# Row-LSTM over a 128x128 image: channels 64-95 of x beside the state h, gates kept in PSUM, GpSimd held until VectorE's reads end, four engines' orders written down

## The chip, the cores and the metric

The kernel runs on one core of a Trainium2 chip. The metric is the device time of one execution in microseconds (us); lower is better. Besides the time, one execution was taken by the hardware profiler; all rows quoted below come from its page and its trace. PE is TensorE's matrix multiply, PEld its weight load, DVE is VectorE, ACT is ScalarE, POOL is GpSimd, SP is SyncE, whose queue issues the DMAs of the loop.

## The reference

```python
# x: (8, 96, 128, 128) = batch, channels, rows, columns
def step(carry, row_in):                       # lax.scan over the 128 rows
    h, c = carry                               # (8, 96, 128) each
    ss = conv1d(h, W_ss, kernel 3, padding 1) + b_ss
    gates = ss + row_in                        # 384 channels
    f, i, o, g = sigmoid, sigmoid, sigmoid, tanh of the four quarters
    c_new = f * c + i * g
    h_new = o * jnp.tanh(c_new)
    return ((h_new, c_new), h_new)

its = conv(group_norm(x), W_is * mask, 1x3) + b_is   # the mask leaves the left tap and a part of the middle one
x = x + scan(step, zeros, its by rows)
```

The rows are a recurrence: row r+1 needs the h of row r. The eight images are independent of each other.

## The kernel before

**Statistics.** The kernel first reads x once (64 DMAs) and takes mean and variance of each channel with VectorE's BN_STATS; two small matmuls sum them by group.

**The recurrence.** The batch is cut into two streams `s` of four images. A step of one stream for one row, here a half-step, handles 96 channels x 4 images x 128 columns. There are 256 of them: 32 blocks `k` of `R` = 4 rows, times two streams, issued alternately, so that one stream's tail can lie beside the other's start. Columns are split in even and odd ones (`J` = 64 each), and the three-tap convolution is computed from three inputs: `vs` = even + odd, `vf` = odd - even, and `vd`, two shifted differences. For each of three gate groups `a`, taken in the order 1, 0, 2, TensorE multiplies `vs` and `vf` into the two halves of one PSUM bank `ps[a]` (called *both* below), ScalarE copies the low half with the bias added into `m` (L258), VectorE writes sum and difference back over the two halves (L259, L260: the *sums*), and TensorE adds three more products on top, from `xn` and twice from `vd` (the *rest*). Every product appears as two matmul records. A bank holds 96 partitions of one sigmoid gate (group 0 is f, 1 is i, 2 is o) and 32 partitions of a third of g.

After the rests ScalarE takes tanh of the g parts (L269) and sigmoid of the others (L270) into SBUF tiles `sf`, `si`, `so`; VectorE forms sf*c (L272), si*g (L273), the new c (L274) and, after ScalarE's tanh of c (L275), h = so*th (L279). From h it makes the next row's `vs` and `vf` (L286, L287), and GpSimd makes `vd` (L288) and adds h onto the rows of x that are stored (L294).

**Inputs from x.** Partitions 96-127 of `vs`, `vf`, `vd` and of the weights hold channels 64-95 of the normalised x, so that they ride along in the same matmuls; GpSimd fills them one block ahead, once per row and stream (L198 normalises, L231 and L232 make sum and difference). Channels 0-63 go into `xn` (L198, L217), also by GpSimd. The buffers hold a whole block of four rows and there are two of each.

**What sets the order.** GpSimd's order is that of the code. The orders of TensorE, ScalarE and VectorE are chosen by the scheduler of the tile framework. All DMAs of the loop are issued by SP: `load_rows` (two copies of 512 KB into `xr`, one buffer per stream), `load` (256 KB and 768 KB into one of two buffers of x) and `store` (768 KB).

Of the kernel before, what the change touches and what calls it, by code (L numbers as in the profile page):

```python
# [7 lines left out]
F32 = mybir.dt.float32  # L8
# [13 lines left out]
def kernel(  # L22
# [26 lines left out]

    nc = tc.nc  # L50
    B, C, H, W = x.shape
    P = 128
# [22 lines left out]

    wt = const.tile([P, 5, 4 * C], F32, name="wt")
    wr = const.tile([P, 3, 4 * C], F32, name="wr")
    nc.scalar.dma_start(wr[0:C], w_ss)
# [15 lines left out]
    nc.vector.tensor_add(wr[0:C, 0, :], wr[0:C, 0, :], wr[0:C, 2, :])  # L94
    nc.vector.tensor_add(wt[0:C, 1, :], wr[0:C, 0, :], wr[0:C, 1, :])
    nc.vector.tensor_sub(wt[0:C, 2, :], wr[0:C, 0, :], wr[0:C, 1, :])
    nc.vector.tensor_scalar_mul(wt[0:C, 1:3, :], wt[0:C, 1:3, :], 0.5)
    nc.vector.tensor_scalar_mul(wt[C:P, 1, :], wr[C:P, 1, :], 0.5)
    nc.vector.tensor_scalar_mul(wt[C:P, 2, :], wr[C:P, 1, :], -0.5)
# [17 lines left out]
    vd = pair([P, R, 2, BH, JP], "vd")  # L117
    vs = pair([P, R, BH, J], "vs")
    vf = pair([P, R, BH, J], "vf")
    xn = pair([P, R, 2, BH, J], "xn")  # L120

    hh = pair([C, 2, BH, JP], "hh")
    xr = [const.tile([P, BH, R * W + 1], F32, tag=f"xr{s}", name=f"xr{s}") for s in range(NH)]
    cs = [const.tile([C, 2, BH, J], F32, tag=f"c{s}", name=f"c{s}") for s in range(NH)]
    for s in range(NH):
        nc.gpsimd.memset(cs[s], 0.0)
        nc.gpsimd.memset(xr[s][:, :, 0:1], 0.0)
        nc.gpsimd.memset(vs[s][0][0:C, 0], 0.0)
        nc.gpsimd.memset(vf[s][0][0:C, 0], 0.0)
        nc.gpsimd.memset(vd[s][0][0:C, 0], 0.0)  # L130
        for i in range(2):
            nc.gpsimd.memset(hh[s][i][:, 0, :, J : J + 1], 0.0)
            nc.gpsimd.memset(hh[s][i][:, 1, :, 0:1], 0.0)
            nc.gpsimd.memset(vd[s][i][C:P, :, 1, :, 0:1], 0.0)
# [84 lines left out]
    def normalise_shared(s, k, j):  # L219

        i = k % 2
        z = vd[s][i][C:P]
        norm(
            strided(z[:, 0, 0, j, :], 0, [(2 * BH * JP, R), (BH * JP + 1, 2), (1, J)]),
            xt[s, k][C:P, j, :, :].rearrange("p r (j t) -> p r t j", t=2),
            C,
            0,
            s * BH + j,
        )
        e, o = z[:, :, 0, j, 0:J], z[:, :, 1, j, 1 : J + 1]  # L230
        nc.gpsimd.tensor_add(vs[s][i][C:P, :, j, :], e, o)  # L231
        nc.gpsimd.tensor_sub(vf[s][i][C:P, :, j, :], o, e)  # L232

    def step(s, k, r):
        i = k % 2
        order = (1, 0, 2)
        HB = BH * J
        ps = [
            ps_pool.tile([P, 2 * HB], F32, tag=f"ps{a}", name=f"ps{a}_{s}_{k}_{r}")
            for a in range(3)  # L240
        ]
        flat = "p b j -> p (b j)"

        def mm(a, half, p, rhs, start=False, stop=False):
            o = ps[a] if half is None else ps[a][:, bass.ts(half, HB)]
# [3 lines left out]

        def gt(n, shape=(C, 2 * HB)):  # L250
            return g_pool.tile(list(shape), F32, tag=n, name=f"{n}_{s}_{k}_{r}")

        for a in order:
            mm(a, 0, 1, vs[s][i][:, r].rearrange(flat), start=True)
            mm(a, 1, 2, vf[s][i][:, r].rearrange(flat))
            m1 = gt(f"m{a}", (P, HB))
            lo, hi = ps[a][:, 0:HB], ps[a][:, HB : 2 * HB]
            nc.scalar.activation(m1, lo, AF.Identity, bias=bias[:, a : a + 1])  # L258
            nc.vector.tensor_add(lo, m1, hi)  # L259
            nc.vector.tensor_sub(hi, m1, hi)  # L260
        for a in order:
            mm(a, None, 4, xn[s][i][:, r].rearrange("p t b j -> p (t b j)"))
            mm(a, 0, 0, vd[s][i][:, r, 1, :, 0:J])
            mm(a, 1, 3, vd[s][i][:, r, 0, :, 0:J], stop=True)

        sg = [gt("sf"), gt("si"), gt("so")]
        g, th = gt("g"), gt("th")
        for a in order:
            nc.scalar.activation(g[a * 32 : (a + 1) * 32], ps[a][C:P], AF.Tanh)  # L269
            nc.scalar.activation(sg[a], ps[a][0:C], AF.Sigmoid)  # L270
        c = cs[s].rearrange("p t b j -> p (t b j)")
        nc.vector.tensor_mul(sg[0], sg[0], c)  # L272
        nc.vector.tensor_mul(g, sg[1], g)  # L273
        nc.vector.tensor_add(c, sg[0], g)  # L274
        nc.scalar.activation(th, c, AF.Tanh)  # L275
        h = hh[s][r % 2]
        h3 = strided(h[:, 0, 0, :], 0, [(BH * JP + 1, 2), (JP, BH), (1, J)])
        shaped = "p (t b j) -> p t b j"
        nc.vector.tensor_mul(  # L279
            h3, sg[2].rearrange(shaped, t=2, b=BH), th.rearrange(shaped, t=2, b=BH)  # L280
        )
        if (k, r) != (NB - 1, R - 1):
            kn, rn = (k, r + 1) if r + 1 < R else (k + 1, 0)
            n = kn % 2
            e, o = h[:, 0, :, 0:J], h[:, 1, :, 1 : J + 1]
# [18 lines left out]
    for s in range(NH):  # L304
        load_rows(s, 0)
        load(s, 0)
# [72 lines left out]
```

## Time and profile before

| quantity | value |
|---|---|
| runs without the profiler | 2945.25, 2950.84, 2955.51 us; median 2950.84 |
| the profiled execution's own time | 2938.35 us |
| its span from first to last instruction | 2936.5 us |
| statistics, up to the first group matmul | 207.28 us |
| first matmul of the recurrence | 224.40 us |
| mean granted TensorE clock | 0.958 |
| mean time from one tanh of c (L275) to the next | 10.55 us |

A line of a group reads: source line, engine, operation, output tile <- input tiles, shapes, count, then the busy time and the mean duration of one in ns, then the time for which the engine was idle just before, with what ended it. A line of the timeline gives start and duration in us, and in brackets the idle time before it. In a timeline line "x2" two records are merged, and a matmul's recorded end is modelled: the distance between the starts of two groups tells the pace better than the durations.

### The profile page before, as it was taken

The page shows a single profiled execution, that of the slowest core. Times are in us where ns is not written, and L with a number is a line of the kernel's source. Part 1 is how long each engine was busy: PE and PEld are TensorE (multiplying, and loading weights), DVE is VectorE, ACT ScalarE, POOL GpSimd, SP SyncE. Part 2 cuts the span into 40 slices and gives each one's busy share as a digit, 9 for nine tenths or more (in the row PEclk, how much of TensorE's full clock was granted, in tenths as well). Part 3 has the DMA queues.
Part 4 walks back from the last instruction along what each step waited for, and adds up shares of the span by engine and source line. Part 5 has one row for each costly group of instructions (what it writes and reads, how often), then busy time and mean ns, then how long its engine had stood idle before and what let it go on. Part 6 is the DMA issues. An engine that isn't in the chain of part 4 may idle for free.

```text
span 2936.5 us, 26168 instructions
## 1 busy us (share of the span) xinstructions
PE 2255.3 (77%) x7688; PEld 1481.7 (50%) x7688; DVE 2074.1 (71%) x3352; ACT 1364.6 (46%) x2564; POOL 1567.7 (53%) x1828
## 2 busy tenths in 40 slices
PE   0008888888888888888888888888888888888887
PEld 0005555555555555555555555555555555555555
DVE  7876766677766766776666677766777776777666
ACT  0005445445554444554454455544444555454445
POOL 0016555665555556555555655555556555555562
PEclk9999999999999999999999999999999999999999
DMA  9992333312233332122333212233332122333300
GB/s 248 259 255 54 79 79 79 79 43 62 54 79 79 79 79 61 44 66 67 79 79 79 68 45 70 56 79 79 79 79 65 44 69 60 79 79 79 79 22 22
DMA packets 103581, 237.76 MB, mean 81 GB/s; under 512 B 6576, under 2 KB 7088, under 8 KB 97296
## 3 DMA queue, kind: packets, MB, share of 16 engines
q1 hardware_dynamic: 102400, 234.91, 32.7%
q10 hardware_dynamic: 1040, 1.18, 0.2%
q8 instruction: 63, 1.03, 0.1%
q14 instruction: 78, 0.64, 0.1%
HBM read 185.73 MB, written 50.33 MB: 80 GB/s over the span
## 4 chain that ended last, share of the span: by engine, by line
DVE 46%; PE 21%; POOL 18%; DMA 5%; ACT 5%; issue 4%; ACTq 0%; POOLq 0%; DVEq 0%
PE ps L246 21%; DVE vf L287 9%; DVE ps L259 8%; DVE vs L286 7%; DVE ps L260 6%; DVE hh L279 6%; DMA xc<-in_x_dram 5%; POOL vd L198 5%; DVE g L273 4%; DVE c L274 4%; POOL vs L231 4%; ACT g L269 4%; POOL x L294 3%; POOL xn L198 2%; POOL vd L288 2%
## 5 line engine op out<-in xcount | busy, mean ns | idle before, releaser
L246 PE MATMUL ps<-xn,wt 128*128 128x512 f32 x1536 | 842.1, 630 | 250.7 <-DVE ps L260 249.4
L269 ACT ACTIVATE g<-ps 32x512 f32<-32x512 f32 x768 | 454.2, 591 | 953.2 <-PE ps L246 953.1
L288 POOL TENSOR_TENSOR vd<-hh 96x512 f32<-96x512 f32 x254 | 263.7, 1038 | 1082.3 <-DVE hh L279 1082.3
L246 PEld LDWEIGHTS ps<-vd,wt 128*128 128x128 f32 x3072 | 582.2, 190 | 411.7 <-issue 370.6
L246 PE MATMUL ps<-vd,wt 128*128 128x256 f32 x3072 | 788.2, 378 | 0.0
L246 PE MATMUL ps<-vs,wt 128*128 128x256 f32 x1536 | 522.5, 425 | 212.0 <-POOL vs L231 212.0
L258 ACT ACTIVATE m<-ps,bias 128x256 f32<-128x256 f32 x768 | 358.0, 466 | 386.6 <-PE ps L246 385.8
L246 PE MATMUL ps<-vf,wt 128*128 128x256 f32 x1536 | 517.6, 422 | 0.0
L259 DVE TENSOR_TENSOR ps<-m,ps 128x256 f32<-128x256 f32 x768 | 309.4, 422 | 274.1 <-ACT m L258 274.1
L246 PEld LDWEIGHTS ps<-xn,wt 128*128 128x128 f32 x1536 | 253.0, 191 | 468.9 <-DVE ps L260 454.9
L246 PEld LDWEIGHTS ps<-vs,wt 128*128 128x128 f32 x1536 | 320.6, 213 | 287.0 <-POOL vs L231 237.4
L273 DVE TENSOR_TENSOR g<-si,g 96x512 f32<-96x512 f32 x256 | 176.3, 689 | 300.4 <-ACT g L269 300.4
L294 POOL TENSOR_TENSOR x<-x,hh 96x512 f32<-96x512 f32 x256 | 377.3, 1474 | 14.1 <-DVE hh L279 14.1
L287 DVE TENSOR_TENSOR vf<-hh 96x256 f32<-96x256 f32 x254 | 380.7, 1499 | 0.0
L246 PEld LDWEIGHTS ps<-vf,wt 128*128 128x128 f32 x1536 | 324.0, 213 | 68.1 <-POOL vf L232 19.7
L198 POOL TENSOR_SCALAR xn<-xr,rstd,nmr 128x512 f32<-128x512 f32 x256 | 247.8, 968 | 199.0 <-DVE nmr L176 198.9
L272 DVE TENSOR_TENSOR sf<-sf,c 96x512 f32<-96x512 f32 x256 | 178.4, 697 | 218.9 <-ACT sf L270 218.9
L260 DVE TENSOR_TENSOR ps<-m,ps 128x256 f32<-128x256 f32 x768 | 325.4, 424 | 8.9
L286 DVE TENSOR_TENSOR vs<-hh 96x256 f32<-96x256 f32 x254 | 294.0, 1157 | 0.0
L231 POOL TENSOR_TENSOR vs<-vd 32x256 f32<-32x256 f32 x256 | 247.5, 967 | 21.3
L198 POOL TENSOR_SCALAR vd<-x,rstd,nmr 32x512 f32<-32x512 f32 x256 | 235.5, 920 | 23.4
L274 DVE TENSOR_TENSOR c<-sf,g 96x512 f32<-96x512 f32 x256 | 207.1, 809 | 8.9
(49 smaller groups left out, 1187.5 us busy)
## 6 DMA issues: line engine op xcount, KB each, us to landing
xr<-in_x_dram SPq DMA_DIRECT2D x128, 512.0 KB, 6.9
xc<-in_x_dram SPq DMA_DIRECT2D x64, 768.0 KB, 9.6
x<-in_x_dram SPq DMA_DIRECT2D x64, 768.0 KB, 9.8
out_dram<-x SPq DMA_DIRECT2D x64, 768.0 KB, 5.3
x<-in_x_dram SPq DMA_DIRECT2D x64, 256.0 KB, 7.3
wr<-in_w_ss_dram ACTq DMA_DIRECT2D x1, 432.0 KB, 7.9
wt<-in_w_ss_dram ACTq DMA_DIRECT2D x2, 144.0 KB, 10.0
wt<-in_w_is_dram ACTq DMA_DIRECT2D x2, 96.0 KB, 4.2
```

The lines of the kernel that those rows point to most:

```text
L198: nc.gpsimd.tensor_scalar(dst, src, rstd[lo:P, layout, b : b + 1], nmr[lo:P, layout, b : b + 1], ALU.mult, ALU.add,)
L231: nc.gpsimd.tensor_add(vs[s][i][C:P, :, j, :], e, o)
L246: nc.tensor.matmul(o, wt[:, p, bass.ts(a, P)], rhs, start=start, stop=stop, skip_group_check=True)
L258: nc.scalar.activation(m1, lo, AF.Identity, bias=bias[:, a : a + 1])
L259: nc.vector.tensor_add(lo, m1, hi)
L260: nc.vector.tensor_sub(hi, m1, hi)
L269: nc.scalar.activation(g[a * 32 : (a + 1) * 32], ps[a][C:P], AF.Tanh)
L274: nc.vector.tensor_add(c, sg[0], g)
L286: nc.vector.tensor_add(vs[s][n][0:C, rn], e, o)
L287: nc.vector.tensor_sub(vf[s][n][0:C, rn], o, e)
L288: nc.gpsimd.tensor_sub(vd[s][n][0:C, rn, :, :, 0:J], strided(h[:, 0, 0, :], 1, [(BH * JP - 1, 2), (JP, BH), (1, J)]), h3,)
L294: nc.gpsimd.tensor_add(xr_, xr_, h3)
```

## The change

There are four edits, and some setup that follows from them.

1. **Channels 64-95 of x treated as channels of h.** `vd`, `vs`, `vf` (for whole blocks) and `hh` go. In their place `hx` holds h in partitions 0-95 and the normalised channels 64-95 of x in partitions 96-127, per row. One pair of VectorE instructions on 128 partitions makes `vs` and `vf` for both, and one GpSimd instruction makes `vd`; the GpSimd sum and difference for x alone (L231, L232) are gone. The weights get rows for it: the right tap of partitions 96-127 is zero.
2. **Gates kept in PSUM.** The sigmoids are written in place into `ps[a]`; the products f*c, i*g, the sum c and the output h read one operand from there. `sf`, `si`, `so` are gone.
3. **GpSimd held.** The GpSimd instruction that makes `vd` gets an added dependence on VectorE's `vf`.
4. **Orders written down.** TensorE, ScalarE, VectorE and GpSimd follow the code. A half-step `now` is interleaved with the end of the one before it, `prev`, which is the other stream's. GpSimd's normalisation is spread over the rows in another way (`OWN`, `SHARED`), and the loads are written stream by stream: blocks 0 and 1 before the loop, block k+2 at the end of block k, where it was the start of block k+1 for both streams together.

```diff
-    for p, tap in ((0, 0), (3, 2)):
-        nc.scalar.dma_start(wt[0:C, p, :], w_ss[:, tap])
-        nc.scalar.dma_start(wt[C:P, p, :], w_is[C2:C, 0])
+    nc.scalar.dma_start(wt[0:C, 3, :], w_ss[:, 2])
+    nc.gpsimd.memset(wt[C:P, 3, :], 0.0)
...
+    hx = pair([P, R, 2, BH, JP], "hx")
...
-        e, o = z[:, :, 0, j, 0:J], z[:, :, 1, j, 1 : J + 1]
-        nc.gpsimd.tensor_add(vs[s][i][C:P, :, j, :], e, o)
-        nc.gpsimd.tensor_sub(vf[s][i][C:P, :, j, :], o, e)
...
+    def inputs(s, row):
+        h = hx[s][row // R % 2][:, row % R]
+        vs, vf = gt("vs", s, row, (P, HB)), gt("vf", s, row, (P, HB))
+        vd = gt("vd", s, row, (P, 2, HB))
+        shaped = "p (b j) -> p b j"
+        e, o = h[:, 0, :, 0:J], h[:, 1, :, 1 : J + 1]
+        nc.vector.tensor_add(vs.rearrange(shaped, b=BH), e, o)
+        last = nc.vector.tensor_sub(vf.rearrange(shaped, b=BH), o, e)
+        diff = nc.gpsimd.tensor_sub(
+            vd.rearrange("p t (b j) -> p t b j", b=BH),
+            strided(h[:, 0, 0, :], 1, [(BH * JP - 1, 2), (JP, BH), (1, J)]),
+            strided(h[:, 0, 0, :], 0, [(BH * JP + 1, 2), (JP, BH), (1, J)]),
+        )
+        tc.add_manual_dep(
+            diff.ins,
+            last.ins.name,
...
+        def sigmoid(self, a):
+            gate = self.ps[a][0:C]
+            nc.scalar.activation(gate, gate, AF.Sigmoid)
+        def forget(self):
+            f = self.ps[0][0:C]
+            nc.vector.tensor_mul(f, f, cs[self.s].rearrange("p t b j -> p (t b j)"))
+        def gated(self):
+            nc.vector.tensor_mul(self.g, self.ps[1][0:C], self.g)
...
+            self.moving = inputs(s, row + 1) if row + 1 < NT else None
+            xo = xt[s, row // R][0:C, :, row % R, :].rearrange("p b (j t) -> p t b j", t=2)
+            nc.gpsimd.tensor_add(xo, xo, h)
...
+    OWN, SHARED = ((0, 1), (2,), (), (3,)), ((), (0, 1), (2, 3), ())
+    def finish(s, row):
+        prepare(s, row)
+        k = row // R
+        if row % R == R - 1:
+            if k + 2 < NB:
+                load_rows(s, k + 2)
+            store(s, k)
+            if k + 2 < NB:
+                load(s, k + 2)
...
+    with tc.manual_schedule(engines={E.PE, E.Activation, E.DVE, E.Pool}):
+        prev = None
+        for row in range(NT):
             for s in range(NH):
+                now = HalfStep(s, row, moving[s])
+                a0, a1, a2 = order
+                now.both(a0)
+                if prev:
+                    prev.tanh(a2)
+                    prev.gated()
+                now.copy(a0)
+                now.sums(a0)
+                if prev:
+                    prev.sigmoid(a2)
+                now.both(a1)
+                now.copy(a1)
+                if prev:
+                    prev.cell()
+                now.sums(a1)
+                now.both(a2)
+                now.copy(a2)
+                now.sums(a2)
+                if prev:
+                    prev.cell_tanh()
+                    prev.output()
+                    moving[prev.s] = prev.moving
+                    finish(prev.s, prev.row)
+                now.rest(a0)
+                now.tanh(a0)
+                now.sigmoid(a0)
+                now.rest(a1)
+                now.tanh(a1)
+                now.sigmoid(a1)
+                now.forget()
+                now.rest(a2)
+                prev = now
```

In the changed kernel `copy`, `sums`, `rest`, `tanh`, `cell` and `cell_tanh` are the instructions of L258, L259 with L260, the products from `xn` and `vd`, L269, L274 and L275 of before; `both` is the pair of products from `vs` and `vf`. TensorE's order of products is the same in both kernels: three *both*, then three *rest*.

VectorE before, in the middle of the recurrence, for one half-step of stream 0 (the four numbers in `ps_0_5_1_3005` are stream, block, row in the block and a running number; the tiles that end in `_5_0_2982` and the like belong to stream 1, one half-step earlier):

```order
L272 TENSOR_TENSOR sf_5_0_2982<-sf_5_0_2982,c_128 96x512
L273 TENSOR_TENSOR g_5_0_2985<-si_5_0_2983,g_5_0_2985 96x512
L274 TENSOR_TENSOR c_128<-sf_5_0_2982,g_5_0_2985 96x512
L259 TENSOR_TENSOR ps_0_5_1_3005<-m_0_5_1_3009,ps_0_5_1_3005 128x256
L259 TENSOR_TENSOR ps_0_5_1_3004<-m_0_5_1_3015,ps_0_5_1_3004 128x256
L260 TENSOR_TENSOR ps_0_5_1_3005<-m_0_5_1_3009,ps_0_5_1_3005 128x256
L279 TENSOR_TENSOR hh_123<-so_5_0_2984,th_5_0_2986 96x2x4x64
L260 TENSOR_TENSOR ps_0_5_1_3004<-m_0_5_1_3015,ps_0_5_1_3004 128x256
L286 TENSOR_TENSOR vs_112<-hh_123 96x256
L287 TENSOR_TENSOR vf_116<-hh_123 96x256
L259 TENSOR_TENSOR ps_0_5_1_3006<-m_0_5_1_3021,ps_0_5_1_3006 128x256
L260 TENSOR_TENSOR ps_0_5_1_3006<-m_0_5_1_3021,ps_0_5_1_3006 128x256
```

VectorE in the changed kernel, the same place (here `ps_0_21_2885` is stream 0, row 21; `ps_1_20` belongs to stream 1's half-step before it):

```order
L304 TENSOR_TENSOR ps_1_20_2830<-ps_1_20_2830,c_114 96x512
L307 TENSOR_TENSOR g_20_2833<-ps_1_20_2831,g_20_2833 96x512
L286 TENSOR_TENSOR ps_0_21_2885<-m_0_21_2892,ps_0_21_2885 128x256
L287 TENSOR_TENSOR ps_0_21_2885<-m_0_21_2892,ps_0_21_2885 128x256
L311 TENSOR_TENSOR c_114<-ps_1_20_2830,g_20_2833 96x512
L286 TENSOR_TENSOR ps_0_21_2884<-m_0_21_2899,ps_0_21_2884 128x256
L287 TENSOR_TENSOR ps_0_21_2884<-m_0_21_2899,ps_0_21_2884 128x256
L286 TENSOR_TENSOR ps_0_21_2886<-m_0_21_2906,ps_0_21_2886 128x256
L287 TENSOR_TENSOR ps_0_21_2886<-m_0_21_2906,ps_0_21_2886 128x256
L325 TENSOR_TENSOR hx_106<-ps_1_20_2832,th_20_2910 96x2x4x64
L241 TENSOR_TENSOR vs_21_2913<-hx_106 128x256
L242 TENSOR_TENSOR vf_21_2914<-hx_106 128x256
```

The sums of gate group 1 moved ahead of the new c, and those of group 2 moved from behind h, `vs` and `vf` to ahead of them: the three instructions that make the next row's input now come last.

GpSimd before, at the end of a block, for row 3 of one stream (`vd_106`, `vs_110` and `vf_114` are block buffers, `x_5_2441` the next block's x):

```order
L288 TENSOR_TENSOR vd_106<-hh_122 96x8x64
L294 TENSOR_TENSOR x_4_1989<-x_4_1989,hh_122 96x2x4x64
L198 TENSOR_SCALAR xn_118<-xr_125,rstd,nmr 128x8x64
L217 MEMSET xn_118 64x4
L198 TENSOR_SCALAR vd_106<-x_5_2441,rstd,nmr 32x4x2x64
L231 TENSOR_TENSOR vs_110<-vd_106 32x4x64
L232 TENSOR_TENSOR vf_114<-vd_106 32x4x64
L198 TENSOR_SCALAR vd_106<-x_5_2441,rstd,nmr 32x4x2x64
L231 TENSOR_TENSOR vs_110<-vd_106 32x4x64
L232 TENSOR_TENSOR vf_114<-vd_106 32x4x64
```

GpSimd in the changed kernel, from row 2 of stream 1 (first three rows) to row 3 of both streams at the end of a block:

```order
L243 TENSOR_TENSOR vd_27_3565<-hx_105 128x512
L332 TENSOR_TENSOR x_6_2813<-x_6_2813,hx_105 96x2x4x64
L194 TENSOR_SCALAR hx_106<-x_7_3249,rstd,nmr 32x4x2x64 x2
L243 TENSOR_TENSOR vd_28_3617<-hx_104 128x512
L332 TENSOR_TENSOR x_6_2755<-x_6_2755,hx_104 96x2x4x64
L194 TENSOR_SCALAR xn_108<-xr_111,rstd,nmr 128x8x64
L213 MEMSET xn_108 64x4
L243 TENSOR_TENSOR vd_28_3675<-hx_106 128x512
L332 TENSOR_TENSOR x_6_2813<-x_6_2813,hx_106 96x2x4x64
L194 TENSOR_SCALAR xn_110<-xr_112,rstd,nmr 128x8x64
```

After the last row of a block there were two normalisations of `vd` with a sum and a difference each; now only one of `xn` and its memset stand there, and the normalisations into `hx` are done by the end of row 2.

More of the change, by code (lines that the diff above doesn't have):

```diff
@@ L248, in mm @@
             )
[L250 to L260, printed above, removed]
@@ L293, in step, with both, copy, sums @@
[L293 to L294 removed]
+        def both(self, a):
+            self.mm(a, 0, 1, self.vs, start=True)
+            self.mm(a, 1, 2, self.vf)
+        def copy(self, a):
+            self.m1 = gt(f"m{a}", self.s, self.row, (P, HB))
+            nc.scalar.activation(
+                self.m1, self.ps[a][:, 0:HB], AF.Identity, bias=bias[:, a : a + 1]
+            )
+        def sums(self, a):
+            lo, hi = self.ps[a][:, 0:HB], self.ps[a][:, HB : 2 * HB]
+            nc.vector.tensor_add(lo, self.m1, hi)
+            nc.vector.tensor_sub(hi, self.m1, hi)
@@ L331 @@
-    for s in range(NH):
-        store(s, NB - 1)
+    for s in range(NH):
+        load_rows(s, 1)
+        load(s, 1)
+    moving = [inputs(s, 0) for s in range(NH)]
+    E = mybir.EngineType
+    with tc.manual_schedule(engines={E.PE, E.Activation, E.DVE, E.Pool}):
+        prev = None
+        for row in range(NT):
+            for s in range(NH):
+                now = HalfStep(s, row, moving[s])
[30 more added lines that the diff above has]
+                prev = now
+        prev.tanh(a2)
+        prev.gated()
+        prev.sigmoid(a2)
+        prev.cell()
+        prev.cell_tanh()
+        prev.output()
+        finish(prev.s, prev.row)
```

148 lines of the change are left out of this document (66 added, 82 removed).

## The prediction

> **What bounds the kernel now.** I read the page first, then the waits, then the timeline of one regular half-step, then that of a block's start.
>
> ```profile
> span 2936.5 us, 26168 instructions
> PE 2255.3 (77%) x7688; PEld 1481.7 (50%) x7688; DVE 2074.1 (71%) x3352; ACT 1364.6 (46%) x2564; POOL 1567.7 (53%) x1828
> DVE 46%; PE 21%; POOL 18%; DMA 5%; ACT 5%; issue 4%; ACTq 0%; POOLq 0%; DVEq 0%
> PEld ps L246 <- DVE ps L260: 454.9, 507, 1.2
> PE ps L246 <- POOL vs L231: 212.0, 64, 14.2
> ```
>
> No engine is full. The chain that ended last is mostly VectorE, though TensorE is the busiest, and TensorE waits for two things: the sums (507 times) and, 64 times, GpSimd's part of `vs` from x. The first is the regular half-step:
>
> ```profile
> 1465.07 0.59 PE L246 MATMUL ps<-vf,wt 128*128 128x256 f32 x2
> 1466.07 0.68 DVE L279 TENSOR_TENSOR hh<-so,th 96x512 f32<-96x512 f32 x1
> 1466.22 1.12 PE L246 MATMUL ps<-xn,wt 128*128 128x512 f32 x2 [0.56 <-DVE ps L260]
> 1466.83 1.04 POOL L288 TENSOR_TENSOR vd<-hh 96x512 f32<-96x512 f32 x1 [3.12 <-DVE hh L279]
> 1467.01 1.15 DVE L286 TENSOR_TENSOR vs<-hh 96x256 f32<-96x256 f32 x1
> 1467.18 1.03 PE L246 MATMUL ps<-vd,wt 128*128 128x256 f32 x4
> 1467.83 1.48 POOL L294 TENSOR_TENSOR x<-x,hh 96x512 f32<-96x512 f32 x1
> 1468.04 1.02 PE L246 MATMUL ps<-xn,wt 128*128 128x512 f32 x2
> 1468.07 1.51 DVE L287 TENSOR_TENSOR vf<-hh 96x256 f32<-96x256 f32 x1
> 1468.90 1.03 PE L246 MATMUL ps<-vd,wt 128*128 128x256 f32 x4
> 1469.51 0.42 DVE L259 TENSOR_TENSOR ps<-m,ps 128x256 f32<-128x256 f32 x1
> 1469.96 0.43 DVE L260 TENSOR_TENSOR ps<-m,ps 128x256 f32<-128x256 f32 x1
> 1470.33 0.10 POOL L217 MEMSET xn<- 64x4 f32 x1
> 1470.45 1.13 PE L246 MATMUL ps<-xn,wt 128*128 128x512 f32 x2 [0.52 <-DVE ps L260]
> 1471.41 1.03 PE L246 MATMUL ps<-vd,wt 128*128 128x256 f32 x4
> 1472.27 0.59 PE L246 MATMUL ps<-vs,wt 128*128 128x256 f32 x2
> 1472.47 0.59 ACT L269 ACTIVATE g<-ps 32x512 f32<-32x512 f32 x1 [1.31 <-PE ps L246]
> 1472.70 0.59 PE L246 MATMUL ps<-vf,wt 128*128 128x256 f32 x2
> 1473.10 0.69 DVE L273 TENSOR_TENSOR g<-si,g 96x512 f32<-96x512 f32 x1 [1.21 <-ACT g L269]
> 1474.26 0.47 ACT L258 ACTIVATE m<-ps,bias 128x256 f32<-128x256 f32 x1 [0.22 <-PE ps L246]
> 1475.58 1.13 PE L246 MATMUL ps<-xn,wt 128*128 128x512 f32 x2 [0.56 <-DVE ps L260]
> ```
>
> A half-step takes 1475.58 - 1466.22 = 9.36 us. The loop is: last rest (1470.45) to tanh (1472.47), g, c, tanh of c, h (1466.07 in the half-step before), `vs`, `vf`, sums of group 2 (1469.51), last rest (1470.45). In it `vs` and `vf` take 1.15 and 1.51 us. They start while GpSimd's `vd` and x-add run and end just after those do: blocked, not long by themselves. How long they would be shows where GpSimd came second:
>
> ```profile
> 239.48 0.42 DVE L286 TENSOR_TENSOR vs<-hh 96x256 f32<-96x256 f32 x1
> ```
>
> TensorE's own pace follows from the starts. A pair of records on 256 columns takes 1472.70 - 1472.27 = 0.43 us; a rest without a wait takes 1468.90 - 1468.04 = 0.86 for `xn` and 1472.27 - 1471.41 = 0.86 for `vd`. Six of the first and three rests make 6 x 0.43 + 3 x 1.72 = **7.74 us**, TensorE's floor for a half-step. The missing 1.62 us are two late starts and about 0.1 us behind each: where the wait has only just ended, `xn` takes 1467.18 - 1466.22 = 0.96 us. The second kind of wait stands at the start of a block:
>
> ```profile
> 224.40 1.22 PE L246 MATMUL ps<-vs,wt 128*128 128x256 f32 x2 [14.15 <-POOL vs L231]
> 238.26 1.22 PE L246 MATMUL ps<-vs,wt 128*128 128x256 f32 x2 [4.09 <-POOL vs L231]
> 1508.72 1.22 PE L246 MATMUL ps<-vs,wt 128*128 128x256 f32 x2 [3.12 <-POOL vs L231]
> 1510.58 1.06 PE L246 MATMUL ps<-vs,wt 128*128 128x256 f32 x2
> 1511.44 1.06 PE L246 MATMUL ps<-vf,wt 128*128 128x256 f32 x2
> 1440.00:1450.00 10.00, 8.92 (x33) 5.84 (x32) 7.92 (x14) 5.70 (x11) 4.15 (x5) 1.00 0.00 1
> 1508.00:1512.00 4.00, 3.28 (x8) 2.61 (x9) 0.58 (x2) 0.47 (x1) 1.36 (x2) 0.50 1.07 213
> 2925.13 1.03 PE L246 MATMUL ps<-vd,wt 128*128 128x256 f32 x4
> ```
>
> TensorE stands for some 3 us, the granted clock falls to 0.50 (second-last window; 1.00 in a regular stretch), and pairs take 0.86 instead of 0.43. From stream 1's first product at 238.26 to the last one's end at 2925.13 + 0.86 = 2925.99 there are 255 half-steps in 2687.7 us. At 9.36 each they would take 2386.8; the other 300.9 us are 62 starts of a block, 4.85 each.
>
> **The change part by part.** It makes the half-step's loop shorter in two ways (order, hold) and takes away the wait at the block's start. I lay one new half-step out from these rows, t = 0 where TensorE starts *both* of group 1, all else in the written order.
>
> TensorE does *both* of 1, 0, 2 until 0.86, 1.72, 2.58 and would then start the first rest. For that the sums of group 1 must be ready, by two paths. First path: tanh of `prev` starts 1472.47 - 1472.27 = 0.20 after its products, 0.20 to 0.79; `gated` follows (0.04 behind, as 1473.10 behind 1472.47 + 0.59) from 0.83 to 1.52. Second: the copy starts 0.26 behind *both* (1474.26 against a pace that ends at 1474.00), from 1.12 to 1.59. So the sums run from 1.62; the second of them starts 0.45 later (1469.96 - 1469.51) and ends at 2.50; TensorE could start at 2.55, as 1470.45 comes 0.06 behind 1469.96 + 0.43. That is **0.03 us before** 2.58: no stall, but a wait that has only just ended, so I count 0.07 of the 0.10 us above. Half-step: 7.74 + 0.07 = **7.81 us**.
>
> The rest has room. On VectorE c runs 2.41 to 3.10, the sums of group 0 end at 3.89 (needed at 4.37), those of group 2 at 4.68 (needed at 6.09), h ends at 5.26, `vs` and `vf` end at 5.71 and 6.06 and are needed at 7.81 and 8.24.
>
> *GpSimd held:* its `vd` starts at 6.1, no longer beside `vs`. Behind it on GpSimd wait the x-add and the normalisations; `vd` is read first 3.4 us into the next half-step, at 11.25, and is done by 7.2. What is late next is `xn` at a block's start: from 1466.83 to 1470.43 the row before took 3.6 us for `vd`, x-add, one `xn` and memset, so 6.1 + 3.6 = 9.7, against the first rest of the next half-step at 7.81 + 2.55 = 10.36. This hides it by 0.66 us; past that each us costs 62 us in all. With nothing gained, `vs` and `vf` of 1.15 and 1.51 us would end at 6.4 and 7.9, still before 7.81 and 8.24: by this sum the order alone would do.
>
> *x beside h:* GpSimd loses L231 and L232 each half-step and TensorE's 64 waits for them go, 300.9 us with the half-clock stretches. Products and their sizes stay the same.
>
> *Gates in PSUM:* no row has such operands on 512 columns.
>
> ```profile
> L260 DVE TENSOR_TENSOR ps<-m,ps 128x256 f32<-128x256 f32 x768 | 325.4, 424 | 8.9
> L272 DVE TENSOR_TENSOR sf<-sf,c 96x512 f32<-96x512 f32 x256 | 178.4, 697 | 218.9 <-ACT sf L270 218.9
> L270 ACT ACTIVATE so<-ps 96x512 f32<-96x512 f32 x256 | 152.4, 595 | 6.3
> ```
>
> For VectorE the bounds are 0.69 (L272, SBUF alone) and 2 x 0.42 = 0.84 (two of L260, which read and write PSUM); L260's 0.42 equals the `vs` of 239.48 on as many columns, so I take 0.69; 0.84 would end `gated` at 1.67 and add 0.05 us a half-step, 13 us. A sigmoid written to PSUM: from 0.47 (the copy) to 1.18 (twice L270), taken as 0.59. ScalarE's sum is 3 x 0.47 + 6 x 0.59 + 0.62 = 5.57, or 7.34 at the upper end, below 7.74 either way: nothing. The Trainium skill, "ScalarE: Activation LUTs", section on the table-load gate, says that ScalarE writes to PSUM faster than to SBUF; by it the sum stays as it is, and no run here shows it yet.
>
> *SP:* four loads and a store per stream and block as before, now stream by stream.
>
> ```profile
> xr<-in_x_dram SPq DMA_DIRECT2D x128, 512.0 KB, 6.9
> x<-in_x_dram SPq DMA_DIRECT2D x64, 768.0 KB, 9.8
> ```
>
> Stream 1's `xr` is issued one half-step after stream 0's, 17.5 on the same count, and queues behind stream 0's `load`, itself behind the store. 9.8 + 6.9 later is 34.2 if they ran one after the other in full, 27.3 if it lands with the slower of the two; GpSimd wants it at 3 x 7.81 + 8.6 = 32.0. GpSimd has 4 us until `vd` is missed, so I cost it at nothing. The setup on VectorE and of the weights lies under the 207 us of statistics: nothing.
>
> *Sum.* GpSimd's eight normalisations and memsets for stream 0 end near 219.4 without L231 and L232; stream 0's first half-step costs 9.6 us as before (half clock); VectorE makes stream 1's first `vs` behind `gated`, and its products start at 231.5 (238.26 before). Then 255 x 7.81 = 1991.6, and the same tail, 2936.5 - 2925.99 = 10.5: span 2233.6, and with 2938.35 - 2936.5 = 1.85 around it **2235.4 us**. The median shown is 12.5 us above the profiled execution; scaled alike (0.4%) this gives **2245 us**.
>
> **The rivals.** *A, the hand-overs at the start bind.* Group 1's sums hang on two hand-overs with 0.03 us to spare. Each 0.1 us more is 25.6 us; at 0.5 the half-step is 8.3 and the time 2370. For it: the bracketed waits above sit at this place today. Against: every hand-over has its row.
>
> *B, the block's start still waits, now for `xn`.* 0.66 us to spare by rows; 1 us too late gives 2245 + 62 = 2307.
>
> *C, the change does not do what it says:* TensorE goes on waiting for the sums as now and only the block's wait goes: 231.5 + 255 x 9.36 + 12.4 = 2631, scaled 2642. Against: the sums of group 2 no longer stand behind `vf`.
>
> *D, slower: the clock.* The floor is TensorE's, so its granted clock now sets the time. At a mean of 0.73 the half-step reaches 7.74 / 0.73 = 10.6, today's mean of 10.54 with the blocks' starts; at 0.50 it is 15.5 and the time about 4190. Half clock came behind idle stretches of 3 us, and the regular stretch with two idle half microseconds per half-step was granted 1.00. The Trainium skill, "TensorE: Matmul & The Clock Gate", section "A second HAM failure mode: psum-queue depth-cycling", says that frequent short idles between groups of matmuls can make the gate oscillate. The row of 1440 to 1450 speaks against that rule here; by it the time would lie between C and this rival's point.
>
> **How the numbers follow.** Forecast 0.65 (2225 to 2275: 7.74 to 7.91 per half-step), A 0.18, B 0.08, C 0.05, D 0.04. The range runs from 2222 to 2330, which takes in B and A up to 0.33 us and leaves out some 0.16. A measurement tells about 0.3% from no change. Faster 0.95 (all but D and a fifth of C, kept for its case that the blocks' waits stay too), same 0.01, slower 0.04.
>
> **What would show it.** Right: first products of successive half-steps 7.8 us apart, TensorE near 98% busy between 240 us and the end, granted clock 1.00, `vs` and `vf` at 0.42, no row of TensorE waiting for GpSimd. A shows as TensorE waiting for the sums more than 0.1 us a half-step, B as TensorE waiting for `xn` 62 times, C as `vs` near 1.15 and 9.36 per half-step, D in the clock. A half-step under 7.74 would make the floor wrong.

## The result, and the profile after

| | median us | lowest to highest | runs |
|---|---|---|---|
| before | 2949.72 | 2945.25 to 2955.51 | 4 |
| changed | 2239.22 | 2237.62 to 2246.42 | 4 |

The ratio is 0.7595, 95% interval 0.7573 to 0.7617: faster by 710 us. The profiled execution of the changed kernel took 2246.42 us, the longest of the four.

First the page of the changed kernel (span, busy time by engine, the chain that ended last), three rows of its waits (time in all, times, longest), and a window (length, busy time and count of PE, PEld, DVE, ACT and POOL, granted clock, share of the DMA engines, GB/s).

```profile
span 2244.6 us, 24459 instructions
PE 2002.9 (89%) x7688; PEld 1441.8 (64%) x7688; DVE 1629.4 (73%) x3354; ACT 1348.8 (60%) x2564; POOL 1027.0 (46%) x1311
PE 89%; DMA 7%; DVE 3%; POOL 0%; issue 0%; ACT 0%; POOLq 0%; DVEq 0%
PE pm L155 <- DVE dq L158: 219.1, 1, 219.1
PEld ps L270 <- DVE ps L287: 32.0, 192, 0.2
PEld ps L270 <- POOL xn L213: 0.2, 1, 0.2
252.00:2230.00 1978.00, 1978.00 (x7607) 1424.16 (x7607) 1446.21 (x3042) 1331.43 (x2537) 1004.23 (x1251) 1.00 0.39 89
```

The chain is now one engine, TensorE, behind 219 us of statistics; before it was VectorE at 46%. The 64 waits for GpSimd's `vs` are gone, and the wait for the sums has shrunk from 454.9 to 32.0 us: 0.17 each in six half-steps of eight (the other two are taken up below). Throughout the recurrence the granted clock was 1.00. Then the timeline of one half-step, from group 1's products to the same place in the next half-step:

```profile
1500.97 0.59 PE L270 MATMUL ps<-vs,wt 128*128 128x256 f32 x2
1501.17 0.59 ACT L296 ACTIVATE g<-ps 32x512 f32<-32x512 f32 x1 [0.53 <-PE ps L270]
1501.79 0.69 DVE L307 TENSOR_TENSOR g<-ps,g 96x512 f32<-96x512 f32 x1 [0.42 <-ACT g L296]
1502.03 0.47 ACT L280 ACTIVATE m<-ps,bias 128x256 f32<-128x256 f32 x1 [0.27 <-PE ps L270]
1502.54 0.43 DVE L286 TENSOR_TENSOR ps<-m,ps 128x256 f32<-128x256 f32 x1
1503.01 0.43 DVE L287 TENSOR_TENSOR ps<-m,ps 128x256 f32<-128x256 f32 x1
...
1503.49 0.30 PEld L270 LDWEIGHTS ps<-xn,wt 128*128 128x128 f32 x2 [0.17 <-DVE ps L287]
1503.56 1.05 PE L270 MATMUL ps<-xn,wt 128*128 128x512 f32 x2
...
1505.53 0.68 DVE L325 TENSOR_TENSOR hx<-ps,th 96x512 f32<-96x512 f32 x1
1506.24 0.43 DVE L241 TENSOR_TENSOR vs<-hx 128x256 f32<-128x256 f32 x1
1506.58 0.42 DVE L242 TENSOR_TENSOR vf<-hx 128x256 f32<-128x256 f32 x1
...
1508.76 0.59 PE L270 MATMUL ps<-vs,wt 128*128 128x256 f32 x2
```

The half-step takes 1508.76 - 1500.97 = 7.79 us; `vs` is ready 2.1 us before TensorE reads it (1506.67 against 1508.76). The only place where TensorE still waits is the first rest: the second sum ends at 1503.44 and the weights for `xn` are loaded from 1503.49.

### The profile page after: what moved, and what is told of

Read it like the earlier page. It is cut to its first block, busy times and chain, and to the rows that moved or that the text cites. A ratio compares the mean times of both kernels' runs of the same rounds, so it can differ in the third digit from the quotient of the medians.

```text
span 2244.6 us, 24459 instructions
## 1 busy us (share of the span) xinstructions
PE 2002.9 (89%) x7688; PEld 1441.8 (64%) x7688; DVE 1629.4 (73%) x3354; ACT 1348.8 (60%) x2564; POOL 1027.0 (46%) x1311
## 4 chain that ended last, share of the span: by engine, by line
PE 89%; DMA 7%; DVE 3%; POOL 0%; issue 0%; ACT 0%; POOLq 0%; DVEq 0%
PE ps L270 89%; DMA xc<-in_x_dram 7%; DVE bst L141 2%; DMA wt<-in_w_ss_dram 0%; DMA wt<-in_w_is_dram 0%; POOL hx L194 0%; POOL xn L194 0%; PE pm L155 0%; POOLq L460 0%; POOL x L332 0%; DVE ps L287 0%; ACT L300 0%; ACT g L296 0%; ACT ps L300 0%; DVE ps L286 0%
## 5 line engine op out<-in xcount | busy, mean ns | idle before, releaser
L243 POOL TENSOR_TENSOR vd<-hx 128x512 f32<-128x512 f32 x256 | 266.1, 1039 | 942.4 <-DVE vf L242 748.5
L270 PE MATMUL ps<-vs,wt 128*128 128x256 f32 x1536 | 458.5, 380 | 11.6 <-DVE vs L241 11.6
L270 PE MATMUL ps<-vf,wt 128*128 128x256 f32 x1536 | 458.2, 380 | 0.0
L300 ACT ACTIVATE ps<-ps 96x512 f32<-96x512 f32 x768 | 442.9, 577 | 16.1
L304 DVE TENSOR_TENSOR ps<-ps,c 96x512 f32<-96x512 f32 x256 | 177.9, 695 | 377.8 <-ACT ps L300 377.8
L332 POOL TENSOR_TENSOR x<-x,hx 96x512 f32<-96x512 f32 x256 | 331.4, 1295 | 9.5 <-DVE hx L325 9.5
L307 DVE TENSOR_TENSOR g<-ps,g 96x512 f32<-96x512 f32 x256 | 175.6, 686 | 106.7 <-ACT g L296 106.7
L194 POOL TENSOR_SCALAR hx<-x,rstd,nmr 32x512 f32<-32x512 f32 x256 | 207.7, 811 | 25.4
L155 PE MATMUL pm<-dq,gm 96*128 96x8 f32 x8 | 2.0, 362 | 220.0 <-DVE dq L158 219.1
L141 DVE BATCH_NORM_STATS2 bst<-xc 96x6 f32<-96x512 f32 x256 | 157.4, 675 | 40.5 <-DMA xc<-in_x_dram 40.5
L325 DVE TENSOR_TENSOR hx<-ps,th 96x512 f32<-96x512 f32 x256 | 173.9, 679 | 0.7 <-ACT th L315 0.7
```

The lines of the kernel that those rows point to most:

```text
L141: nc.vector.bn_stats(bst[:, k * (CH // SN) + j, :], xc[0:C, bass.ts(j, SN)])
L194: nc.gpsimd.tensor_scalar(dst, src, rstd[lo:P, layout, b : b + 1], nmr[lo:P, layout, b : b + 1], ALU.mult, ALU.add,)
L243: diff = nc.gpsimd.tensor_sub(vd.rearrange("p t (b j) -> p t b j", b=BH), strided(h[:, 0, 0, :], 1, [(BH * JP - 1, 2), (JP, BH), (1, J)]), ...
L270: nc.tensor.matmul(o, wt[:, p, bass.ts(a, P)], rhs, start=start, stop=stop, skip_group_check=True)
L300: nc.scalar.activation(gate, gate, AF.Sigmoid)
L304: nc.vector.tensor_mul(f, f, cs[self.s].rearrange("p t b j -> p (t b j)"))
```

## The experiments

All kernels are written as edits of the changed kernel (`after`) or of the one before. Three edits recur. Without the third, VectorE's and ScalarE's orders are the scheduler's; TensorE's order of products stays as it was. Where the gates go back to SBUF, VectorE's products read the SBUF tiles, too.

```diff
 # "hold", taken out:
-        tc.add_manual_dep(diff.ins, last.ins.name, ...)
 # "PSUM", taken out (f, i, o each):
-            gate = self.ps[a][0:C]
-            nc.scalar.activation(gate, gate, AF.Sigmoid)
+            self.sg[a] = gt(("sf", "si", "so")[a], self.s, self.row)
+            nc.scalar.activation(self.sg[a], self.ps[a][0:C], AF.Sigmoid)
 # "order", taken out (one half-step after the other, as in before):
-    with tc.manual_schedule(engines={E.PE, E.Activation, E.DVE, E.Pool}):
+    with tc.manual_schedule(engines={E.Pool}):
```

With "x" for channels 64-95 beside h (and all the setup that follows from it, the moved loads among it), this gives every combination of the other three on top of x. Medians in us; the ratio is to the kernel before, run on the same chip; the half-step is the mean distance of ScalarE's tanh of c from one to the next, in the middle of the loop (10.58 in the kernel before). Without x only the hold was run.

| label | x | hold | PSUM | order | us | ratio, 95% interval | half-step |
|---|---|---|---|---|---|---|---|
| hold_only | - | yes | - | - | 2900.40 | 0.9841 [0.9822, 0.9859] | 10.42 |
| x_only | yes | - | - | - | 2461.25 | 0.8349 [0.8312, 0.8385] | 8.68 |
| x_hold | yes | yes | - | - | 2489.08 | 0.8443 [0.8400, 0.8487] | 8.77 |
| x_psum | yes | - | yes | - | 2627.35 | 0.8912 [0.8870, 0.8954] | 9.32 |
| no_order | yes | yes | yes | - | 2627.31 | 0.8916 [0.8903, 0.8929] | 9.31 |
| x_order | yes | - | - | yes | 2302.06 | 0.7809 [0.7774, 0.7843] | 8.06 |
| no_psum | yes | yes | - | yes | 2288.27 | 0.7765 [0.7752, 0.7778] | 8.00 |
| no_hold | yes | - | yes | yes | 2240.92 | 0.7605 [0.7594, 0.7616] | 7.80 |
| after_again | yes | yes | yes | yes | 2239.87 | 0.7597 [0.7585, 0.7610] | 7.803 |

### The hold

**no_hold.** The changed kernel without the hold.

> The changed kernel without the added dependence of GpSimd's vd on VectorE's vf; the other three edits stay. My theory: with the written order the hold is not needed. vs and vf are blocked again (near 1.15 and 1.51 us instead of 0.43), but vf then ends some 7.9 us into a half-step and is read at 8.2, so the half-step stays at 7.80 us and the time at 2239 us, within 0.3%. Rival, the hold is what carries the gain: vf comes too late by 0.3 us or more, TensorE waits for VectorE at the head of each half-step, 2320 us or above.

It took 2240.92 us; with the hold it is 2239.22 and 2239.87. The timeline shows that the blocking is back for `vf`, though not for `vs`, and harms nothing:

```profile
1464.19 0.68 DVE L319 TENSOR_TENSOR hx<-ps,th 96x512 f32<-96x512 f32 x1
1464.90 0.42 DVE L241 TENSOR_TENSOR vs<-hx 128x256 f32<-128x256 f32 x1
1465.04 1.18 POOL L243 TENSOR_TENSOR vd<-hx 128x512 f32<-128x512 f32 x1 [2.39 <-DVE hx L319]
1465.24 1.26 DVE L242 TENSOR_TENSOR vf<-hx 128x256 f32<-128x256 f32 x1
1466.19 1.47 POOL L326 TENSOR_TENSOR x<-x,hx 96x512 f32<-96x512 f32 x1
```

`vd` takes 1.18 us instead of 1.04 beside `vs`, then `vf` takes 1.26 instead of 0.42 beside `vd`. `vf` is still done over a microsecond before TensorE reads it. In this order the hold is worth nothing.

**hold_only.** The kernel before with the same dependence added, and nothing else.

> The kernel before with nothing but the added dependence: GpSimd's part of vd from h waits for VectorE's vf. Theory: vs and vf fall to 0.42 us and the regular half-step to 8.5 us; the wait at a block's start stays and grows by as much as the half-step shrinks, since GpSimd's work there is the same: 238 + 255 x 8.5 + 62 x 5.7 + 10 = 2770 us, 2700 to 2850. Rival, GpSimd starts later and only moves the wait: 2930 us or more.

It took 2900.40 us: right in sign, but 47 us gained (2947.39 before, on the same chip) where some 180 were expected, and outside the expected range. By place in the eight half-steps of a block, six went from 9.36 to 9.39 us down to 8.58 to 8.93, and the two with the block's start went from 14.2 up to 15.1 and 15.3. A block's start in the timeline of before, first `vd` and then the last part of `vs` from x for which TensorE waits:

```profile
1500.00 1.04 POOL L288 TENSOR_TENSOR vd<-hh 96x512 f32<-96x512 f32 x1 [5.07 <-DVE hh L279]
1507.70 0.96 POOL L231 TENSOR_TENSOR vs<-vd 32x256 f32<-32x256 f32 x1
```

The same in hold_only, from the h of that row, and a row of its waits:

```profile
1465.13 0.68 DVE L279 TENSOR_TENSOR hh<-so,th 96x512 f32<-96x512 f32 x1
1466.89 1.04 POOL L288 TENSOR_TENSOR vd<-hh 96x512 f32<-96x512 f32 x1 [2.08 <-DVE vf L287]
1474.69 0.64 POOL L231 TENSOR_TENSOR vs<-vd 32x256 f32<-32x256 f32 x1
PE ps L246 <- POOL vs L231: 305.8, 64, 14.1
```

Held back, `vd` starts 1.08 us behind the end of h (1466.89 - 1465.81); before it is 0.08. GpSimd's work for x stands behind it, and so its last `vs` is ready 9.50 us behind h where it was 8.75, in the mean over the blocks. TensorE's wait there grows from 212.0 to 305.8 us. That is the rival's mechanism: the hold moved the wait, and took back 2.05 of the 3.3 us that the six other half-steps had gained in a block. It moved the collision, too: some of this work now falls beside VectorE's c, which takes 0.93 us in the mean where 0.69 is its length alone.

**x_only** and **x_hold** ask the same where x rides along and nothing else is changed.

> Only channels 64 to 95 of x beside h (with the new inputs and the new spread of GpSimd's normalisation); no hold, gates in SBUF, orders of the three engines left to the scheduler. Theory: the waits at a block's start go, the regular half-step stays at 9.36 us: 231.5 + 255 x 9.36 + 12.4 = 2630 us, 300 less than before. Rival, the block's wait only changes its name (xn or vd for vs): above 2850 us.

> x beside h and GpSimd held; gates in SBUF, orders left to the scheduler. Theory: vs and vf fall to 0.43 us, the loop over h loses 1.8 us and the first rest's wait binds: 8.5 us a half-step, 2420 us. Rival, VectorE's other instructions with two SBUF operands then meet GpSimd: 9 us or more, above 2540 us.

Both missed. x_only was 169 us faster than I said, and x_hold 28 us slower than x_only where I expected a gain of some 200 (against the 2630 expected of x_only). Timeline of x_only at the end of a half-step:

```profile
1463.63 0.68 DVE L320 TENSOR_TENSOR hx<-so,th 96x512 f32<-96x512 f32 x1
1463.78 1.13 PE L265 MATMUL ps<-xn,wt 128*128 128x512 f32 x2 [0.56 <-DVE ps L282]
1464.48 1.73 POOL L243 TENSOR_TENSOR vd<-hx 128x512 f32<-128x512 f32 x1 [3.78 <-DVE hx L320]
1464.56 0.41 DVE L241 TENSOR_TENSOR vs<-hx 128x256 f32<-128x256 f32 x1
1464.90 0.41 DVE L242 TENSOR_TENSOR vf<-hx 128x256 f32<-128x256 f32 x1
```

`vs` and `vf` take 0.41 us with no hold at all, and GpSimd's `vd` is the one that is stretched (1.73 for 1.04). Before, `vd` started 0.08 us after h had ended and `vs` took 1.15; here it starts 0.17 after h. So the edit that moves channels of x, with its setup, already does what the hold is for. That, and no wait for GpSimd at a block's start, is what x_only gains: before, six half-steps of 9.37 and two of 14.2 make a mean of 10.58, here it is 8.68, and 255 x 1.90 = 484 of the 485 us by which it beats the kernel before on the same chip. Why `vd` starts 0.09 us later was not tried.

In two of the eight half-steps of a block, GpSimd's pair of normalisations (one row below) stands behind one of `xn`, and meets VectorE's i*g and c. First x_hold, then the same place of x_only:

```profile
1463.23 2.57 POOL L194 TENSOR_SCALAR hx<-x,rstd,nmr 32x512 f32<-32x512 f32 x2
1464.29 0.79 DVE L308 TENSOR_TENSOR g<-si,g 96x512 f32<-96x512 f32 x1 [0.43 <-ACT g L297]
1465.12 1.22 DVE L312 TENSOR_TENSOR c<-sf,g 96x512 f32<-96x512 f32 x1
1467.39 1.13 PE L271 MATMUL ps<-xn,wt 128*128 128x512 f32 x2 [1.16 <-DVE ps L288]
```

```profile
1442.14 2.56 POOL L194 TENSOR_SCALAR hx<-x,rstd,nmr 32x512 f32<-32x512 f32 x2
1443.50 0.69 DVE L302 TENSOR_TENSOR g<-si,g 96x512 f32<-96x512 f32 x1
1444.22 1.04 DVE L306 TENSOR_TENSOR c<-sf,g 96x512 f32<-96x512 f32 x1
1446.31 1.13 PE L265 MATMUL ps<-xn,wt 128*128 128x512 f32 x2 [0.88 <-DVE ps L282]
```

The pair meets c in both kernels. With the hold it comes later in the half-step, i*g is stretched as well and c by 0.18 us more; the sums stand behind c, and TensorE waits 1.16 us for them, 0.88 in x_only. These two half-steps take 9.15 and 9.17 us where x_only has 8.88 and 8.89: 64 x 0.28 = 18 of the 28 us. As in hold_only, the hold moved a collision and did not remove it.

### The gates in PSUM

**no_psum** and **x_order** keep the gates in SBUF under the written order, with and without the hold; **x_psum** moves them to PSUM under the scheduler's order.

> The changed kernel with the sigmoids written to SBUF tiles again; order, hold and the new inputs stay. Theory: the products i*g, f*c and the sum c then read two SBUF operands while GpSimd is at its x-add and normalisations, which in the changed kernel last to 1.5 to 3.1 us into the next half-step; i*g starts at 0.83 and is blocked by what is left of one GpSimd instruction, so the first sums come 0.3 to 0.6 us later: 8.1 to 8.4 us a half-step, 2310 to 2390 us, with i*g well above its 0.69 us. Rival, the PSUM operands matter for nothing since GpSimd's blocks miss these instructions: 2239 us within 0.3%.

> x beside h and the written orders; no hold, gates in SBUF. Theory: as with the hold and SBUF gates, i*g meets GpSimd at the head of each half-step: 8.1 to 8.6 us, 2310 to 2440 us. Rival, the order alone gives all: 2239 us within 0.3%.

> x beside h and the gates in PSUM; no hold, orders left to the scheduler. Theory: vs and vf stay blocked and in the loop, 9.3 us a half-step, 2600 to 2640 us. Rival, the PSUM gates alone shorten the loop by more than 0.5 us: below 2500 us.

no_psum took 2288.27 us, 49 more than with PSUM. That is less than I expected, below the range, and in another place. Its timeline:

```profile
1464.44 1.29 POOL L333 TENSOR_TENSOR x<-x,hx 96x512 f32<-96x512 f32 x1
1464.81 1.47 DVE L305 TENSOR_TENSOR sf<-sf,c 96x512 f32<-96x512 f32 x1 [1.52 <-ACT sf L301]
1466.20 0.68 DVE L308 TENSOR_TENSOR g<-si,g 96x512 f32<-96x512 f32 x1
```

I had said that i*g would be blocked. It is f*c, by the x-add: 1.47 us here and 1.54 in the mean of the loop, instead of 0.69. i*g therefore starts late, and with it the sums and the first rest. With both operands of f*c and i*g in SBUF each of them can meet GpSimd; with one in PSUM (695 and 686 ns in the changed kernel's groups) none was stretched.

x_order took 2302.06 us, 8 below its range. There f*c and i*g are both stretched, to 1.11 and 1.01 us in the mean, so i*g met GpSimd as expected. Beside it no_psum, with the hold, is 14 us faster (2302.06 - 2288.27), on another chip and with intervals that just overlap; `vf` took 1.26 us in x_order and 0.42 in no_psum.

x_psum's number was as expected by luck, for another reason: `vs` and `vf` take 0.41, so nothing is blocked, yet it is 166 us *slower* than x_only. Its timeline, in the half-step that starts at 1461.57:

```profile
1463.12 0.69 DVE L305 TENSOR_TENSOR c<-ps,g 96x512 f32<-96x512 f32 x1
1464.52 0.69 DVE L319 TENSOR_TENSOR hx<-ps,th 96x512 f32<-96x512 f32 x1
1465.13 0.42 DVE L281 TENSOR_TENSOR ps<-m,ps 128x256 f32<-128x256 f32 x1
1465.60 1.13 PE L264 MATMUL ps<-xn,wt 128*128 128x512 f32 x2 [1.27 <-DVE ps L281]
```

The scheduler put h ahead of the second sum of group 1. h waits for the tanh of c, the sum waits behind h, and TensorE stands 1.27 us.

### The order

**no_order.** The changed kernel with the scheduler's orders.

> The changed kernel with the orders of TensorE, ScalarE and VectorE left to the scheduler and the code written half-step by half-step; hold, PSUM gates and the new inputs stay, GpSimd's order is that of the code. The scheduler puts the sums of group 1 behind the new c again. Theory: TensorE's first rest then starts near 3.3 us instead of 2.6 after the first product, so 7.74 + 0.7 + 0.1 = 8.5 us a half-step, 2420 us. Rival, hold and PSUM alone carry the gain: 2239 us within 1%. Other rival, the order carries all of it: 9.36 us a half-step, 2630 us.

2627.31 us, the same as x_psum (2627.35), with VectorE's instructions in the same order; not the 2420 of my theory, but the number of the second rival. The written order is worth 388 us once x, PSUM and the hold are there.

**sig_first.** Every order stays written; one ScalarE instruction, the sigmoid of group 2, moves ahead of the copy of group 1.

```diff
                 now.both(a0)
                 if prev:
                     prev.tanh(a2)
                     prev.gated()
-                now.copy(a0)
-                now.sums(a0)
-                if prev:
                     prev.sigmoid(a2)
+                now.copy(a0)
+                now.sums(a0)
```

> The changed kernel with one swap on ScalarE: the sigmoid of group 2 of the half-step before stands ahead of the copy of group 1. Theory: the copy starts at 1.34 instead of 1.12 after the first product, the sums end at 2.72, TensorE starts its first rest at 2.77 plus the 0.1 us behind a wait: 8.03 us a half-step, 0.23 more than the 7.80 measured, +59 us: 2298 us, between 2285 and 2310. Rival, the half-step is TensorE's own pace with slack elsewhere: no change, 2239 us within 0.3%.

2329.82 us, ratio 0.7909 [0.7897, 0.7921], 8.158 us a half-step: 91 us for one instruction, 32 more than expected and outside the range. Timeline of the half-step that starts at 1460.78:

```profile
1460.98 0.59 ACT L296 ACTIVATE g<-ps 32x512 f32<-32x512 f32 x1 [0.53 <-PE ps L270]
1461.61 0.57 ACT L300 ACTIVATE ps<-ps 96x512 f32<-96x512 f32 x1
1462.20 0.98 ACT L280 ACTIVATE m<-ps,bias 128x256 f32<-128x256 f32 x2
1463.65 1.13 PE L270 MATMUL ps<-xn,wt 128*128 128x512 f32 x2
```

The copy starts 1.42 us into the half-step, not 1.34, and the first rest at 2.87 where the changed kernel has 2.59. The sum that gave 1.34 had left out the gaps between ScalarE's instructions (1461.61 is 0.04 behind the end of the tanh). The first rest is 0.10 us later than that sum had it; the other 0.03 of the 0.13 by which the half-step was missed were not traced.

**dve_order.** Only VectorE's and GpSimd's orders are written.

```diff
-    with tc.manual_schedule(engines={E.PE, E.Activation, E.DVE, E.Pool}):
+    with tc.manual_schedule(engines={E.DVE, E.Pool}):
```

> Only VectorE's and GpSimd's orders are written; TensorE's and ScalarE's are the scheduler's. TensorE's order comes out as in the changed kernel, and ScalarE's differs in one place: the sigmoid of group 2 stands ahead of the copy of group 1's first sum. Theory: VectorE's order carries the edit, and the one swap costs what it cost alone in sig_first: 8.16 us a half-step, 2330 us (2315 to 2345). Rival 1: ScalarE's or TensorE's written order carries it, and the time is that of no_order or above, 2600 us and more. Rival 2: the swap is made good by something else, 2239 us.

2331.08 us, ratio 0.7915 [0.7902, 0.7928], 8.158 us a half-step: sig_first again, as expected. With VectorE's order written, the scheduler's order of ScalarE comes out as in sig_first, and TensorE's as in all the others. So of the 388 us VectorE's order carries 296 and ScalarE's one swap the other 91.

**late_rest.** What is left is the wait of 0.17 us at the first rest. Here the last rest moves behind the next half-step's first *both*, so that TensorE has 1.72 us more to do before the sums of group 1 are wanted.

```diff
                 now.both(a0)
                 if prev:
-                    prev.tanh(a2)
-                    prev.gated()
+                    prev.rest(a2)
                 now.copy(a0)
                 now.sums(a0)
-                if prev:
-                    prev.sigmoid(a2)
                 now.both(a1)
-                now.copy(a1)
                 if prev:
+                    prev.tanh(a2)
+                    prev.gated()
+                    prev.sigmoid(a2)
                     prev.cell()
+                now.copy(a1)
                 now.sums(a1)
                 now.both(a2)
                 now.copy(a2)
-                now.sums(a2)
...
                     finish(prev.s, prev.row)
+                now.sums(a2)
                 now.rest(a0)
...
                 now.forget()
-                now.rest(a2)
                 prev = now
+        prev.rest(a2)
```

> The changed kernel with the last rest of a half-step moved behind the first pair of products of the next (TensorE), the sums of group 1 ahead of i*g and those of group 2 behind h, vs and vf (VectorE), tanh and sigmoid of group 2 behind the copy of group 1 (ScalarE). The sums of group 1 then have 1.7 us more before they are needed. Theory: TensorE never waits and the half-step falls from 7.80 to 7.74 or 7.75 us: 13 to 15 us less, 2225 us against the changed kernel on the same chip. Rival, vs of the next half-step, read at 7.74 and made by about 7.6, comes too late: 2260 us or more.

2229.34 us (2228.46 to 2231.98), ratio 0.7565 [0.7555, 0.7576], on the chip and in the comparison of after_again (2239.87, 2235.17 to 2243.90; 0.7597 [0.7585, 0.7610]): the fastest kernel here. It is 10.5 us faster than the changed one, where 13 to 15 were expected: 0.5%, with intervals that don't meet. Its timeline:

```profile
1501.29 0.59 PE L270 MATMUL ps<-vs,wt 128*128 128x256 f32 x2
1502.16 1.02 PE L270 MATMUL ps<-xn,wt 128*128 128x512 f32 x2
...
1505.61 1.02 PE L270 MATMUL ps<-xn,wt 128*128 128x512 f32 x2
```

*Both* of group 1 starts at 1501.29, the half-step before's last rest follows at 1502.16, and this half-step's first rest starts at 1505.61: 4.32 us behind its own products instead of 2.59, and without a wait. Its half-step is 7.755 us at all eight places, and between 252 and 2200 us no gap is left between TensorE's matmuls: this is its floor. 255 x (7.803 - 7.755) = 12 us is what the loop gained.

**after_again** repeats the changed kernel, unaltered, for that comparison.

> The changed kernel unaltered, as the neighbour of the run with the moved rest: 2239 us within 0.3%.

## Why the prediction was right, step by step

**The floor and the one hand-over** carried it. 7.74 us was worked out from rounded starts; late_rest, whose matmuls wait for nothing in the loop, shows 7.755. The forecast added 0.07 for a wait that has only just ended; 7.79 - 7.755 = 0.035 was paid. The floor was 0.015 too low and this term too high, so part of the close agreement is two small misses that cancel. The places inside the half-step came out as laid out: `gated` 0.82 us behind TensorE's start (forecast 0.83), copy 1.06 (1.12), sums from 1.57 (1.62) to 2.47 (2.50), first rest 2.59 (2.58 or a little after). Forecast 7.81, measured 7.803. sig_first shows how thin the margin of rival A was: 0.36 us of delay on ScalarE gave 0.35 more per half-step. (The forecast's own rows gave 2.50 + 0.06 = 2.56, so it had 0.02 us to spare at the first rest, not 0.03.)

**The waits at a block's start** went, with the half clock: TensorE waited 0.2 us for `xn` in all, so rival B is out. Two half-steps in eight, those of a block's first row, take 7.85 and not 7.79: the first weight load for `xn` starts 0.11 us behind the end of the sums there and 0.05 elsewhere. That costs 64 x 0.06 = 4 us. In the trace TensorE's queue has one more instruction at these places, which does nothing but wait for the sums; the load behind it waits for GpSimd, whose `xn` of the new block is read here for the first time. No run takes that instruction out, but in late_rest, where the sums are early, all eight places are equal.

**The hold at nothing** ("by this sum the order alone would do") held beside PSUM: no_hold. With the gates in SBUF the order alone did not do (x_order, 2302 us). Rival **C**, TensorE waiting on at 9.36 us a half-step, is out by the 7.79 us of the timeline.

**PSUM operands** were priced right where the range ran from 0.69 to 0.84 and from 0.47 to 1.18:

```profile
L300 ACT ACTIVATE ps<-ps 96x512 f32<-96x512 f32 x768 | 442.9, 577 | 16.1
L304 DVE TENSOR_TENSOR ps<-ps,c 96x512 f32<-96x512 f32 x256 | 177.9, 695 | 377.8 <-ACT ps L300 377.8
L307 DVE TENSOR_TENSOR g<-ps,g 96x512 f32<-96x512 f32 x256 | 175.6, 686 | 106.7 <-ACT g L296 106.7
```

0.695 and 0.686 us for VectorE, 0.577 for ScalarE, against 0.697 and 0.595 before. The Trainium skill's rule that ScalarE writes faster to PSUM ("ScalarE: Activation LUTs", "Step-by-step: what each stage is for") agrees, by 18 ns. But the layout gave this edit no worth, and no_psum gives it 49 us. It looked at GpSimd beside `vs` and `vf` alone, and not beside f*c, i*g and c.

**The head** was the one term off by more than 2 us: stream 1's first products at 231.5 were forecast, and 244.5 came. 11.8 us of it is the statistics, which ended at 219.1 in this execution and at 207.3 before; over all the profiles of this study they ended between 207.3 and 219.5. after_again's span of 2238.1 had 212.7. The profiled execution took 11.0 us more than the sum of 2235.4. The scaling by 0.4%, taken from a profiled execution of before that was shorter than the others, has no support here, where it was the longest; that the median lies between the sum (3.8 above it) and the scaled 2245 (5.8 below it) is luck.

**The clock** (D) stayed at 1.00 over 1978 us. The Trainium skill's rule on depth-cycling ("TensorE: Matmul & The Clock Gate", "A second HAM failure mode: psum-queue depth-cycling") expects an oscillation at frequent short idles. The changed kernel hardly tests it, since by the row its matmuls are busy for all of the 1978.00 us. x_psum does: TensorE stands 1.27 us in every half-step of 9.3 us, and the granted clock was 1.00 there between 300 and 2200 us, so the oscillation of that rule does not show here.

What the prediction did not see is how the edits hang together. It named two causes of the 9.36 us, blocked `vs` and `vf` and the sums of group 2 behind them, and gave the first to the hold and the second to the order. x_only shows that the first went with x alone, and x_psum that PSUM without an order of its own costs 166 us. For x alone the layout gives 2631 us (C), some 300 us less than before; measured it was 485 less on the same chip. The written order with PSUM brought another 220 (x_only to no_hold), and the hold 2, which is within the noise. The order is worth 159 us with the gates in SBUF (x_only to x_order) and 386 with them in PSUM (x_psum to no_hold). The total came out right because the forecast laid out the half-step of the changed kernel whole, and did not add up the shares of its edits.

## What to carry to other kernels

Write down the whole half-step with its hand-overs from the rows of the old trace; if the busiest engine's own pace comes out as the sum, price the edits by what they move at the one hand-over that is left. Where two engines stretch each other's instructions, first ask whether anything waits for the stretched one: in hold_only and x_hold the hold only moved the collision to the next pair. An edit that changes durations by nothing can still change a scheduler's order by 166 us, so look at the order beside the durations.

## What the runs showed that was not expected

Which of two colliding instructions is stretched turned on about 0.1 us. In 253 of 254 half-steps of before, `vd` is recorded 0.16 to 0.18 us ahead of `vs`, and stretches it from 0.42 to 1.15 us. In 251 of 256 of x_only it is recorded 0.07 to 0.11 us ahead, and is itself stretched, from 1.04 to 1.73. (`vd` also has 128 partitions there in place of 96; no run separates the two.) The Trainium skill, "SBUF — State Buffer", section "Who interferes with whom", lets the one that issues first block the other; the recorded start does not always tell which that was. How much it is stretched is steady: it ends behind the other's end by its own length less 0.13 to 0.15 us, as if it began only when the other was all but done. `vs` of before (own 0.42) ended 0.29 behind `vd`, `vd` of x_only (own 1.04) 0.90 behind `vf`, f*c of no_psum (own 0.69) 0.55 behind the x-add. So the price of such a collision can be read from the first one's end and the other's own length.
